# Graph edges on a clock of TensorE's work: one wait per indirect transfer, two gathers to one scatter

## The chip, the cores and the metric

The kernel runs on one core of a Trainium2 chip. The metric is device time in microseconds of one launch; the median of the runs before the change is 2226.0 us (three runs: 2226.4, 2224.77, 2226.0). The engines are named as in the profile: PE (TensorE, matrix products), PEld (its weight loads), DVE (VectorE), ACT (ScalarE), POOL (GpSimd, which here issues the indirect transfers), SP (SyncE, which issues most weight loads).

## The reference, cut to what matters

The program is a two-layer network over 625 nodes of width 1024 and 10,000 edges. The change lies in the first layer, which adds the results of a graph attention and of a linear attention to `x`. The graph attention is the part that has edges:

```python
x = x * rsqrt(mean(x*x) + EPS) * rms_w;  x = x @ W_down          # (625, 256)
xl = (x @ Wl).reshape(n, 4, 64);  xr = (x @ Wr).reshape(n, 4, 64)
msg = xl[src] + xr[dst]                                           # one row per edge
e = einsum('ehd,hd->eh', leaky_relu(msg, 0.2), att)               # 4 scores per edge
p = exp(e - segment_max(e, dst)[dst])
alpha = p / (segment_sum(p, dst)[dst] + 1e-16)
out = segment_sum(alpha[..., None] * xl[src], dst)                # then out @ W_up
```

Beside it, from the same normalised rows, runs a linear attention with four 1024x1024 matrices (`W_q`, `W_k`, `W_v`, `W_o`). A feed-forward block follows, and then a second layer with dense graph products, attention and a mixture of experts.

## The kernel before, in words

All of the first layer is written in an order made by hand (`manual_schedule`): on each engine the instructions run in the order in which the Python code emits them.

**What the edges need.** The rows of `xl` and `xr` (625 rows of 256 floats) lie in DRAM as `xl_d` and `xr_d`. The 10,000 edges are cut into 79 columns of 128 (the last has 16). Each column needs three indirect transfers, which POOL issues: a gather of 128 rows of `xl_d` (tile `ga`), a gather of 128 rows of `xr_d` (tile `gb`), both at line 611, and a scatter of the 128x4 scores into a dense DRAM `table` of 625x625x4 at line 631. That makes 237 transfers. A group is two columns (`G = 2`), so there are 40 groups. Between gather and scatter DVE scores a group: add (L621), times `att` with the rectifier (L591), sum (L592), clip (L594). ACT then takes the exponential (L598). Five pairs of `ga` and `gb` rotate, and so a gather of group g also waits until the score of group g-5 has read its tile. A scatter waits until the scatter before it has landed, as both write `table`.

**What TensorE does meanwhile.** The same stretch holds the linear attention: ten `key` and ten `value` groups (`pk`, `pv`, eight matmuls each), 79 counting steps (`pct`, five bf16 matmuls each, which count how often each pair of nodes occurs), the states (`pkv`), eight queries (`pq`) with their answers (`pd`, `po`), and the output product (`px`, in `mixed`, L745). An fp32 matmul shows as two rows in the trace. The queries' first group needs the PSUM banks that the last `value` group leaves when DVE has read it (L286).

**What sets the order of the edge work.** `one_beat` emits one beat for group g: the self loops for five of the beats, the scores of group g-`lags[0]`, the exponentials of group g-`lags[1]`, and then, for each column of the group, the gather of `ga`, a scatter of group g-`lags[2]`-1 if one is left, the gather of `gb`, and a scatter of group g-`lags[2]`. The lags are 4, 5, 6. `work(us)` is called after each piece of TensorE's work with an estimate of its time and emits a beat once the sum has passed 2.0 + 5.2 us per beat for the first six beats and 8.6 us per beat after that. Only the first transfer of a beat waits for TensorE: for the last matmul that had been emitted by then (`latest["pe"]`). Before the output product the lags become 1, 1, 2. What is left after `mixed(2)` is emitted in one go (`while chunks: one_beat()`).

**What comes next.** When all scatters have landed, POOL loads `table` back in blocks (`load_table`, tile `tb`). DVE multiplies each by the counts (`weigh`, tile `pT`, L841), and TensorE multiplies that with the rows (`sums`, `pg`). The table's columns, the feed-forward block and the second layer follow.

Of the kernel before, what the change touches and what calls it, by code (L numbers as in the profile page):

```python
# [53 lines left out]
def attempt(ctx: ExitStack, tc: tile.TileContext, w: dict, out: bass.AP, shifted: bool):  # L54

    nc = tc.nc
# [10 lines left out]
    def ps2(name):  # L67
        return psums[-1][0].tile([128, 2, 512], FP, tag="ps2", name=name, bufs=3)
# [58 lines left out]
    def group(dst, pairs):  # L127

        for i, (lhsT, rhs) in enumerate(pairs):
            made = nc.tensor.matmul(dst, lhsT=lhsT, rhs=rhs, start=(i == 0), stop=(i == len(pairs) - 1))  # L130
        latest["pe"] = made.ins.name

    latest = {}

    def behind(ins, name):

        tc.add_manual_dep(ins.ins, name, mybir.DependencyInfo(mybir.DependencyClass.Sync,
                                                              mybir.DependencyReason.DATA), reason="pace")
        return ins
# [11 lines left out]
    def nodes(t):  # L151
        return slice(t * P, (t + 1) * P)
# [203 lines left out]
    with ExitStack() as st0:  # L356
# [8 lines left out]
        with ExitStack() as edges:  # L365
# [22 lines left out]
            def load_edges():  # L388
                for dst, name in ((si, "src"), (di, "dst")):
# [15 lines left out]
                              in_=none.unsqueeze(1).to_broadcast([128, 28, 440]))  # L405
# [43 lines left out]
            def count():  # L449

                if part["held"] or part["done"] == EN:
                    return False
                lo, hi, t = counting[part["done"]]
                part["held"] = 2 * (t == hi - 1)

                def prep():
                    while len(made_ahead) < min(8, EN - t):
                        one_hot()
                    hold["hot"] = made_ahead.pop(0)
                    part["done"] += 1  # L460

                def pe():
                    od, os = hold["hot"]
                    if t == lo:
                        part["pc"] = psums[-1][0].tile([128, NT, 512], FP, tag="pct", name="pct", bufs=1)
                    for j in range(NT):
                        made = nc.tensor.matmul(part["pc"][:P, j, :HN], lhsT=os[:, nodes(j)],
                                                rhs=od[:, :HN], start=(t == lo), stop=(t == hi - 1))
                    latest["pe"] = made.ins.name

                def decode():
                    for j in range(0, NT, 2):
                        js = slice(j, min(j + 2, NT))
                        n = js.stop - j
                        low, high, v = CT[:, js, 0:HN], CT[:, js, HN:NP], part["pc"][:P, js, :HN]
                        low_r, high_r = CTr[:, js, 0:HN], CTr[:, js, HN:NP]
                        u = pool.tile([P, 2, HN], FP, tag="u", name="u", bufs=1)[:, 0:n, :]

                        nc.vector.tensor_scalar(u, v, 1728.0 if shifted else 2047.0, BIG, op0=ALU.subtract, op1=ALU.add)
                        nc.vector.tensor_scalar(u, u, BIG, None, op0=ALU.subtract)  # L480
                        if lo == 0:
                            nc.vector.tensor_tensor(low_r, v, u, op=ALU.subtract)
                            nc.vector.tensor_scalar(high_r, u, 1.0 / 4096, None, op0=ALU.mult)
                        else:
                            nc.vector.scalar_tensor_tensor(high_r, u, 1.0 / 4096, high, op0=ALU.mult, op1=ALU.add)
                            nc.vector.tensor_tensor(u, v, u, op=ALU.subtract)
                            nc.vector.tensor_tensor(low_r, low, u, op=ALU.add)
                    if hi == EN:

                        for s in range(NT):  # L490
                            nc.vector.tensor_tensor(CTr[:, s, nodes(s)], CT[:, s, nodes(s)], ident[:P, :P],
                                                    op=ALU.add)

                do(prep, pe, decode if t == hi - 1 else None)
                return True

# [103 lines left out]
            es = pool.tile([128, EN, 4], FP, name="es")  # L600
            G = 2
            groups = [(lo, min(G, EF - lo), 128) for lo in range(0, EF, G)] + [(EF, 1, ER)]
            ab = {}

            def gather(g, j, side):
                lo, n, p = groups[g]
                if j == 0 and side == 0:
                    ab[g] = [pool.tile([128, G, 256], FP, tag=k, name=k, bufs=5) for k in ("ga", "gb")]
                if j < n:
                    src, ix = ((xl_d, si), (xr_d, di))[side]  # L610
                    got = nc.gpsimd.indirect_dma_start(  # L611
                        out=ab[g][side][0:p, j, :], out_offset=None, in_=src[:, :],
                        in_offset=bass.IndirectOffsetOnAxis(ap=ix[0:p, lo + j:lo + j + 1], axis=0))
                    if j == 0 and side == 0 and "pe" in latest:
                        behind(got, latest["pe"])

            def score_group(g):
                lo, n, p = groups[g]
# [5 lines left out]
            chunks = [(g, j) for g, (lo, n, p) in enumerate(groups) for j in range(n)]  # L624

            def scatter(last):

                if chunks and chunks[0][0] <= min(last, beat["raised"] - 1):
                    g, j = chunks.pop(0)
                    lo, n, p = groups[g]  # L630
                    nc.gpsimd.indirect_dma_start(  # L631
                        out=table[:, :],
                        out_offset=bass.IndirectOffsetOnAxis(ap=at[0:p, lo + j:lo + j + 1], axis=0),
                        in_=es[0:p, lo + j, :], in_offset=None)

            own = pool.tile([P, NT, 4], FP, name="own")
            linear = pool.tile([P, NT, 4], FP, name="linear")
# [29 lines left out]

            beat = dict(us=0.0, g=0, scored=0, raised=0)  # L670
            lags = [4, 5, 6]

            def scores(last):
                while beat["scored"] <= min(last, len(groups) - 1):
# [3 lines left out]
            def raise_all(last):  # L678
                while beat["raised"] <= min(last, beat["scored"] - 1):
                    lo, n, p = groups[beat["raised"]]  # L680
                    exp(es[0:p, lo:lo + n, :])
                    beat["raised"] += 1

            def one_beat():
                g = beat["g"]
                beat["g"] += 1
                if 5 <= g < NT + 5:
                    self_loops(g - 5)
                if lags[1] > lags[0]:
                    raise_all(g - lags[1])  # L690
                    scores(g - lags[0])
                else:
                    scores(g - lags[0])
                    raise_all(g - lags[1])
                for j in range(G):
                    if g < len(groups):
                        gather(g, j, 0)
                        scatter(g - lags[2] - 1)
                        gather(g, j, 1)
                    scatter(g - lags[2])  # L700

            def work(us):
                beat["us"] += us

                while beat["us"] >= 2.0 + 5.2 * min(beat["g"], 6) + 8.6 * max(beat["g"] - 6, 0) and chunks:
                    one_beat()

            work(0.0)
            states = []
            for c in range(2):  # L710
                if c:
# [27 lines left out]
            def mixed(t, ks=range(KC), keep=None, then=None, paced=True, cs=(0, 1)):  # L739
                for c in cs:  # L740
                    def pe(c=c):
                        if c == 0 and ks[0] == 0:
                            hold["px", t] = ps2("px1")
                        for k in ks:
                            made = nc.tensor.matmul(hold["px", t][:P, c, :], lhsT=oT[:, k, nodes(t)], rhs=wo[c](k),  # L745
                                                    start=(k == 0), stop=(k == KC - 1 and keep is not None))
                        latest["pe"] = made.ins.name

                    def after():
                        px = hold.pop(("px", t))  # L750
                        for c in range(2):
                            nc.vector.tensor_tensor(keep[:, c, :], px[:P, c, :], bo[c][:P], op=ALU.add)

                    do(None, pe, after if keep is not None and c == 1 else None)
                    if then is not None and c == 0:
                        then()
                    if paced:
                        work(0.87 * len(ks))
# [29 lines left out]
            for m in range(KC):  # L788
# [5 lines left out]
                if m < 3:  # L794
# [3 lines left out]
                                      in_=w[("w_gate", "w_up", "w_down")[m]].rearrange("(k p) n -> p k n", p=128))  # L798
# [7 lines left out]
            made = [gu[:, :, 0:256], gu[:, :, 256:512], dn]  # L806
# [468 lines left out]
    for b in range(NB_MIN, NB):  # L1275
        nc.gpsimd.dma_start(out=y_d[b * 128:(b + 1) * 128, :].rearrange("p (a n) -> p a n", a=4),
                            in_=zero.unsqueeze(1).to_broadcast([128, 4, 256]))
# [694 lines left out]
```

## Time and profile before

| | us |
|---|---|
| median of three runs | 2226.0 |
| the profiled execution, its own time | 2228.76 |
| its span, as the profile draws it | 2227.0 |
| PE busy in the span | 2112.5 (95%) |
| POOL busy in the span | 341.4 (15%) |
| POOL, `ga` gathers, 79 rows | 79.7 (1009 ns each) |
| POOL, `gb` gathers, 79 rows | 81.8 (1036 ns each) |
| POOL, scatters, 79 rows | 84.2 (1066 ns each) |
| stretch 57 to 158: PE / DVE / POOL busy of 101 | 91.25 / 69.67 / 67.80 |
| stretch 158 to 259: of 101 | 99.02 / 59.60 / 66.27 |
| stretch 259 to 377: of 118 | 101.43 / 69.97 / 73.92 |
| stretch 377 to 445: of 68 | 45.57 / 41.67 / 38.37 |
| stretch 445 to 475: of 30 | 16.23 / 14.62 / 10.10 |
| stretch 475 to 640: of 165 | 147.94 / 98.86 / 5.25 |

A row of the timeline reads: start, duration, engine, line, operation, output<-inputs, count, and in brackets how long the engine sat idle before it and what ended that. "issue" means that the profile shows nothing that was waited for, "remote" a semaphore whose sender it can't name.

### The profile page before, as it was taken

How to read it: one execution, taken by the hardware profiler on the slowest of the kernel's cores; microseconds unless marked ns; L12 is line 12 of the kernel's file. 1: busy time of each engine (PE TensorE's matmuls, PEld its weight loads, DVE VectorE, ACT ScalarE, POOL GpSimd, SP SyncE). 2: the span in 40 equal slices, each digit the busy share in tenths (PEclk: the TensorE clock that was granted, in tenths of full speed). 3: DMA queues.
4: the chain of work that ended last, by engine and by line, in shares of the span. 5: the costliest groups of instructions: out<-in, count | busy, mean ns of one | idle time of the engine just before them, and what ended most of it. 6: DMA issues, size and time to landing. Idle time of an engine off the chain costs nothing. (4 is left out here: it accounts for less than half of the span.)

```text
span 2227.0 us, 17363 instructions
## 1 busy us (share of the span) xinstructions
PE 2112.5 (95%) x6934; PEld 1209.9 (54%) x6934; DVE 713.3 (32%) x1214; ACT 194.1 (9%) x354; POOL 341.4 (15%) x349
## 2 busy tenths in 40 slices
PE   8899799578899999999999999999999999999998
PEld 6466375245444777754445767557744444444443
DVE  5765467557623560000113133322011111111112
ACT  2000010001211100000000111100000000000000
POOL 1666656610000020210000000110000000000011
PEclk9999899878999999999999999999999999999999
DMA  9226252071122110231213111021099987997742
GB/s 299 77 62 209 59 182 81 25 212 33 38 85 71 52 38 1 85 142 38 76 38 104 38 38 38 20 103 61 34 347 337 331 325 282 327 331 286 275 144 92
DMA packets 145848, 301.62 MB, mean 135 GB/s; under 512 B 12370, under 2 KB 22436, under 8 KB 145754
## 3 DMA queue, kind: packets, MB, share of 16 engines
q1 hardware_dynamic: 123700, 244.23, 30.7%
q0 software_dynamic: 17376, 46.42, 7.1%
q10 hardware_dynamic: 4678, 9.72, 1.4%
q8 instruction: 58, 0.95, 0.2%
q14 instruction: 36, 0.29, 0.0%
HBM read 277.49 MB, written 22.84 MB: 135 GB/s over the span
## 5 line engine op out<-in xcount | busy, mean ns | idle before, releaser
L130 PE MATMUL pu<-w,xgT 128*128 128x512 f32 x768 | 333.9, 593 | 1.9 <-DVE xgT L1266 1.9
L130 PEld LDWEIGHTS pu<-w,xgT 128*128 128x128 f32 x768 | 144.0, 190 | 174.8 <-issue 171.7
L130 PE MATMUL pyb<-w,hb 128*128 128x512 f32 x384 | 174.3, 599 | 2.5 <-ACT yb L105 2.1
L130 PE MATMUL pq<-xnT,w 128*128 128x313 f32 x512 | 139.6, 432 | 13.8 <-DVE v L286 13.0
L130 PE MATMUL pk<-w,xnT 128*125 128x512 f32 x320 | 143.2, 599 | 3.3 <-issue 2.8
L130 PE MATMUL pv<-w,xnT 128*125 128x512 f32 x320 | 142.2, 597 | 1.5 <-issue 1.1
L130 PE MATMUL p<-tT,w 128*128 128x313 f32 x512 | 136.3, 428 | 0.4 <-DVE tT L1266 0.4
L130 PEld LDWEIGHTS pq<-xnT,w 128*128 128x128 f32 x512 | 98.2, 193 | 53.5 <-DVE v L286 13.8
L130 PEld LDWEIGHTS pyb<-w,hb 128*128 128x128 f32 x384 | 69.8, 189 | 90.9 <-issue 74.8
L1806 DVE TENSOR_TENSOR su<-pu,su 128x512 f32<-128x512 f32 x24 | 16.6, 692 | 314.6 <-ACT su L1805 314.6
L130 PEld LDWEIGHTS p<-tT,w 128*128 128x128 f32 x512 | 96.8, 190 | 37.9 <-issue 1.2
L130 PEld LDWEIGHTS pk<-w,xnT 128*125 128x125 f32 x320 | 59.8, 189 | 77.0 <-issue 76.1
L130 PEld LDWEIGHTS pv<-w,xnT 128*125 128x125 f32 x320 | 59.9, 189 | 75.4 <-issue 72.6
L1789 POOL DMA_INDIRECT xg<-rows_d,slots x12 | 11.4, 946 | 524.8 <-PE pxg L1796 449.0
L631 POOL DMA_INDIRECT table<-es,at x79 | 84.2, 1066 | 49.4 <-issue 26.2
L611 POOL DMA_INDIRECT ga<-xl_d,si x79 | 79.7, 1009 | 74.8 <-issue 33.2
L611 POOL DMA_INDIRECT gb<-xr_d,di x79 | 81.8, 1036 | 25.3 <-issue 22.8
L745 PE MATMUL px<-w,oT 128*125 128x512 f32 x160 | 69.8, 594 | 2.9 <-DVE x L909 2.0
L130 PE MATMUL px<-w,hT 128*125 128x512 f32 x160 | 70.3, 592 | 0.0
L130 PE MATMUL px<-w,oT 128*125 128x512 f32 x160 | 70.3, 592 | 0.0
L130 PE MATMUL ph<-meanT,w 128*128 128x313 f32 x256 | 70.1, 426 | 0.0
L130 PE MATMUL ph<-xnT,w 128*128 128x313 f32 x256 | 70.0, 427 | 0.0
(366 smaller groups left out, 2459.9 us busy)
## 6 DMA issues: line engine op xcount, KB each, us to landing
w<-in_eW_dram SPq DMA_DIRECT2D x144, 1024.0 KB
w<-in_L_Wk_dram SPq DMA_DIRECT2D x8, 1024.0 KB
w<-in_L_Wv_dram SPq DMA_DIRECT2D x8, 1024.0 KB
w<-in_L_Wq_dram SPq DMA_DIRECT2D x8, 1024.0 KB
w<-in_L_Wo_dram SPq DMA_DIRECT2D x8, 1024.0 KB
w<-in_W_self_dram SPq DMA_DIRECT2D x8, 1024.0 KB
w<-in_W_neigh_dram SPq DMA_DIRECT2D x8, 1024.0 KB
w<-in_sW_dram SPq DMA_DIRECT2D x8, 1024.0 KB
```

Of the source, the lines that this page charges most:

```text
L130: made = nc.tensor.matmul(dst, lhsT=lhsT, rhs=rhs, start=(i == 0), stop=(i == len(pairs) - 1))
L611: got = nc.gpsimd.indirect_dma_start(out=ab[g][side][0:p, j, :], out_offset=None, in_=src[:, :], in_offset=bass.IndirectOffsetOnAxis(ap=ix ...
L631: nc.gpsimd.indirect_dma_start(out=table[:, :], out_offset=bass.IndirectOffsetOnAxis(ap=at[0:p, lo + j:lo + j + 1], axis=0), in_=es[0:p, l ...
L745: made = nc.tensor.matmul(hold["px", t][:P, c, :], lhsT=oT[:, k, nodes(t)], rhs=wo[c](k), start=(k == 0), stop=(k == KC - 1 and keep is no ...
L1789: nc.gpsimd.indirect_dma_start(out=xg, out_offset=None, in_=rows_d[:, :], in_offset=bass.IndirectOffsetOnAxis(ap=slots[:, b:b + 1], axis=0))
L1806: nc.vector.tensor_tensor(su, pu[:, 0, :], su, op=ALU.mult)
```

## The change

A clock of TensorE's work is kept while the program is emitted: every matmul adds its estimated time to `pe_time` and leaves a mark (`passed`). A 128x512 fp32 matmul counts 0.87 us, one of 313 columns 0.53, one of the counting step 0.135. Each of the 237 transfers now gets its own wait (`in_time`): for the first matmul whose mark has reached `due`, which starts 1.5 us after the first mark of the stage and grows by 1.38 us with each transfer. A beat holds, for each column, the gather of `ga`, the gather of `gb` and one scatter; the second scatter is gone. The lags are 2, 3, 5 and still become 1, 1, 2 ahead of the output product. `work` emits a beat once the clock has passed the due times of all its transfers, and its argument is no longer read.

```diff
@@ group, and the clock
+            passed(made, 0.0017 * max(dst.free_size(), 154))
-        latest["pe"] = made.ins.name
-
-    latest = {}
+    pe_time = [0.0]
+    marks = []
+
+    def passed(made, us):
+        pe_time[0] += us
+        marks.append((pe_time[0], made.ins.name))
@@ count
-                    latest["pe"] = made.ins.name
+                        passed(made, 0.135)
@@ gather
-                    if j == 0 and side == 0 and "pe" in latest:
-                        behind(got, latest["pe"])
+                    in_time(got)
@@ scatter
-                    nc.gpsimd.indirect_dma_start(
+                    in_time(nc.gpsimd.indirect_dma_start(
...
-            beat = dict(us=0.0, g=0, scored=0, raised=0)
-            lags = [4, 5, 6]
+            beat = dict(g=0, scored=0, raised=0, due=pe_time[0] + 1.5)
+            lags = [2, 3, 5]
+
+            def in_time(made):
+                name = next((name for us, name in marks if us >= beat["due"]), None)
+                if name is not None:
+                    behind(made, name)
+                beat["due"] += 1.38
@@ one_beat
                     if g < len(groups):
                         gather(g, j, 0)
-                        scatter(g - lags[2] - 1)
                         gather(g, j, 1)
                     scatter(g - lags[2])
@@ work
-                beat["us"] += us
-                while beat["us"] >= 2.0 + 5.2 * min(beat["g"], 6) + 8.6 * max(beat["g"] - 6, 0) and chunks:
+                while chunks and pe_time[0] >= beat["due"] + 1.38 * (4 * (beat["g"] < len(groups)) + 2 * (beat["g"] > lags[2])):
                     one_beat()
-            work(0.0)
@@ mixed
-                        latest["pe"] = made.ins.name
+                            passed(made, 0.87)
```

`behind(ins, name)` is unchanged: it makes `ins` wait for the named instruction.

More of the change, by code (lines that the diff above doesn't have):

```diff
@@ L630, in scatter @@
                     lo, n, p = groups[g]
-                    nc.gpsimd.indirect_dma_start(
+                    in_time(nc.gpsimd.indirect_dma_start(
                         out=table[:, :],
                         out_offset=bass.IndirectOffsetOnAxis(ap=at[0:p, lo + j:lo + j + 1], axis=0),
-                        in_=es[0:p, lo + j, :], in_offset=None)
+                        in_=es[0:p, lo + j, :], in_offset=None))
             own = pool.tile([P, NT, 4], FP, name="own")
```

## The prediction

> **What bounds the kernel now.** I read the busy times by stretch first, to find where PE stands still, then PE's timeline around those places, then POOL's timeline over the same time. PE is the bound (95% of the span). In the stage of the edges it works from 45.01 us (first `pk`) to 422.57 (end of the `px` row below), and its next matmul waits:
>
> ```profile
> 394.86 27.71 PE L745 MATMUL px<-w,oT 128*125 128x512 f32 x64
> 454.23 0.68 PE L130 MATMUL pg<-xl,pT 125*125 125x65 f32 x2 [31.66 <-DVE pT L841]
> ```
>
> The `pT` that it waits for needs the loaded table, and the table needs the last scatter. POOL's timeline shows how late the transfers end:
>
> ```profile
> 384.86 0.96 POOL L611 DMA_INDIRECT ga<-xl_d,si  x1 [8.50 <-PE px L745]
> ...
> 422.00 1.12 POOL L631 DMA_INDIRECT table<-es,at  x1 [0.75 <-issue]
> 423.43 2.29 POOL L611 DMA_INDIRECT gb<-xr_d,di  x1 [0.30 <-issue]
> 426.02 1.73 POOL L631 DMA_INDIRECT table<-es,at  x1 [0.30 <-issue]
> 429.67 1.56 POOL L631 DMA_INDIRECT table<-es,at  x1 [1.91 <-ACT es L598]
> 432.64 2.31 POOL L631 DMA_INDIRECT table<-es,at  x1 [1.41 <-DMA table<-es,at]
> 436.82 0.96 POOL L631 DMA_INDIRECT table<-es,at  x1 [1.88 <-issue]
> 439.18 0.96 POOL L631 DMA_INDIRECT table<-es,at  x1 [1.39 <-DMA table<-es,at]
> 442.03 0.85 POOL L631 DMA_INDIRECT table<-es,at  x1 [1.90 <-issue]
> 444.54 0.90 POOL L173 DMA_DIRECT2D tb<-table  x1 [1.66 <-issue]
> ```
>
> Two numbers follow. From 422.00 to 442.03 there are seven steps of 2.86 us, as each scatter waits for the one before it. From the last scatter to the first `pg` it is 454.23 - 442.03 = 12.2 us. The first row shows why the end is late: with 32 transfers still to come after it, POOL is made to wait 8.50 us for a beat.
>
> The second loss lies inside the stage. By the change's own clock (read off the code) PE's work from the first `pk` to the last `px` is 344.1 us; the trace has 422.57 - 45.01 = 377.6. So 33.4 us are lost, 13.0 of them in one place:
>
> ```profile
> 252.29 7.03 PE L130 MATMUL pv<-w,xnT 128*125 128x512 f32 x16
> 272.33 10.21 PE L130 MATMUL pq<-xnT,w 128*128 128x313 f32 x32 [13.01 <-DVE v L286]
> ```
> ```profile
> 271.59 0.69 DVE L286 TENSOR_TENSOR v<-pv,bv_t 125x512 f32<-125x512 f32 x1 [12.73 <-remote]
> ```
> ```profile
> 267.61 0.99 POOL L631 DMA_INDIRECT table<-es,at  x1 [0.30 <-issue]
> 271.82 0.96 POOL L611 DMA_INDIRECT ga<-xl_d,si  x1 [3.23 <-remote]
> ```
>
> By its rows the `pv` group ended at 259.3, yet DVE, which only needs that group here, starts 12.3 us later, and POOL's wait ends with it. PE's signals arrive late. The same shows at 80.67, 227.01 and 351.75 (6.9, 11.1 and 3.6 us late). Each time POOL had issued for 21 to 40 us with gaps of 0.44 or less, and the signal came 2.1 to 3.0 us after POOL's last row. At 77 to 81 and 99 to 110 PE's own rows stretch to one per 0.7 or 1.4 us. Whether POOL's unbroken run holds the signals back, or only waits for them too, this trace can't tell.
>
> **The change, part by part.** *Earlier places.* In the built program the last gather waits for clock 312.6, where before it waited for 330.2; transfer 227, the last that has a gather just ahead of it, waits for 313.4. With PE's loss unchanged that is 45.0 + 313.4 + 33.4 = 391.8, and 1.0 for its turn gives 392.8.
>
> *Can POOL keep up?* From 57 to 376 there are 204 transfers, busy 207.8 us, with 0.30 between rows: 1.32 us each against 1.38 on the clock. The first starts at 57.64 in both (it waits for the rows of `xl_d`), so 227 end at 57.6 + 299.6 = 357.2, and some 19 us of waits for landings and scores in that stretch make 376. That leaves 16 us to 391.8, so TensorE's clock decides, not POOL.
>
> *The tail.* The extra scatter is gone, so scatters stay five groups behind and ten stand alone after transfer 227 (before, seven). 10 x 2.86 = 28.6, so the last starts at 421.4. The row-to-row bounds are 2.36 (436.82 to 439.18) and 4.18 (432.64 to 436.82), that is 24 to 42 us; I take the mean of the seven. DVE's three ternary passes (11.2 us) fall on this tail as they did before, so their effect is in the mean. [...] The rows agree: 1.56 to 2.31 us for a transfer beside those passes, 0.85 to 0.96 after them. Were all ten to fall under the passes, at (432.64 - 426.02)/2 = 3.3 a step, the sum would be 4.5 us higher.
>
> *From the last scatter on.* 421.4 + 12.2 = 433.6 for the first `pg`, against 454.23: 20.6 us less. PE still idles 11.0 us. Its granted clock was 0.78 from 420 to 430 and 0.50 until 470, and an 11 us gap cools it too, so no gain is counted for a warm start. What follows moves as a whole, as its loads start from these same events.
>
> *Shorter lags.* A score stands two beats after its gathers instead of four. Two beats and the beat's own 8.28 us, less 5.5 to the fourth gather and about 4 for issue and landing, leave 15 us of cover. POOL starts 11 us behind its places (57.64 against 46.5), and in the weight loads near 180 a scatter takes 6.8 to 7.3 us (169.41, 176.18, 183.48) against 4.14 on the clock. If the lag passes 15 us, DVE stands at the add, with `kb`, `kf` and `v` behind it in its queue and PE behind those. I price it at 0, bounds 0 and 5. Exponentials one beat after scores let ACT wait less; no price.
>
> *The waits.* On POOL's queue everything behind a waiting transfer waits too: other transfers, one memset, at the end the table loads. PE's signals in the stage rise from 117 to 331 (counted in the built program). A signal has no visible price: counting rows with one per five matmuls take 4.16/30 = 0.139 us against 0.135 on the clock, so at most 214 x 0.02 = 4 us, at least 0; I take 0. The 91 more wait instructions on POOL: rows with several waits show the same 0.30 gap as rows with none (98.12, 60.58), and 16 us of cover stand over them. [...]
>
> *PE's 33.4 us.* POOL now stops at the first late signal instead of running on to its next beat. At 259 it issued seven rows after the group had ended. If the signal comes 3 us after POOL's last row and POOL stops at once, 12.3 us late becomes about 4, which saves 8. I take half, 4.0, since POOL often lags and then runs on. Bounds: a saving of 16.8 (beyond it POOL's 376 decides) and a loss of 33.4 (as much again).
>
> **Sum.** 2227.0 - 20.6 - 4.0 = 2202.4 for a span. The median stands 1.0 below the span here (the execution's own 2228.76 stands 1.8 above), so **2201**.
>
> **The rivals.** *Signals come in time* (0.17): pauses spread over all transfers end the late signals. POOL then decides: 376 + 1 + 28.6 + 12.2 = 417.8 for `pg`, 36.4 less, a median of 2190. For it: no late signal from 158 to 195, where POOL has gaps of 1 to 4 us. Against: the new gaps are 0.06 us on average.
>
> *The scatter chain takes the place* (0.15): POOL drops behind in the weight loads (about 3 us per scatter, as above) and doesn't recover at 0.06 a transfer, and transfer 227 comes 10 to 17 us late: 2211 to 2218. Against: PE's losses give POOL time.
>
> *TensorE is held back more, slower* (0.25): before, a beat ended in a pause when POOL was on time; now POOL rests 0.06 us per transfer. If an unbroken run is what makes signals late, then 327 us at one episode per 22 us are 15 episodes. The six so far cost 5.6 each; at 4 each the loss is 60, 27 us more: 2226 - 20.6 + 27 = 2232. It decides from a loss of 54 us (33.4 + 20.6). Against: each wait stops POOL at once, and 384.86 to 422, a transfer per 1.6 us, shows no late signal.
>
> *The change doesn't do what it says*: in the built program all 237 transfers wait for a matmul, in steps of 0.9 to 1.9 us of the clock. Dropped.
>
> **How the numbers follow.** My forecast has 0.43; its own range is 2194 to 2208. No change is what a measurement can't tell, within 0.2% or 4.5 us; it takes 0.03 from the scatter chain and 0.03 from the slow case. Faster is 0.43 + 0.17 + 0.12 = 0.72, same 0.06, slower 0.22. The range reaches down to the first rival with scatters at 2.5 a step (2186) and up to the slow case with some more loss: 2184 to 2238.
>
> **What would show it.** Last gather near 389, last scatter near 417, first `pg` near 430, with some 11 us of idle PE before it instead of 31.66; no transfer waiting longer than about 3 us but for signals or landings; lone scatters 2.4 to 3.3 apart. Wrong would be: PE's end of `px` well past 423, rows one per 0.7 or 1.4 us in many places, or DVE's L621 waiting for gathers before 380.

## The result and the profile after

| | before | after |
|---|---|---|
| median of 12 runs each, us | 2226.20 (2222.62 to 2229.49) | 2225.33 (2220.86 to 2232.87) |
| ratio, 95% interval | | 1.0002 (0.9989 to 1.0014) |
| profiled execution: span, us | 2227.0 | 2228.1 |
| end of `px` before the first `pg` | 422.57 | 438.87 |
| TensorE's loss (that end, less the first `pk`, less 344.1) | 33.5 | 49.7 |
| start of transfer 227 / last scatter | 417.83 / 442.03 | 412.37 / 443.80 |
| first `pg`, and PE's idle time before it | 454.23, 31.66 | 455.76, 16.89 |

There is no difference that can be told from none; 25 us less were forecast. Later runs on other chips show that this is not the whole answer: on a chip where the kernel before takes 2196 us the change is slower, 1.0060 (1.0040 to 1.0079).

PE's timeline of the changed kernel at the end of the stage (start, duration, engine, line, operation, count, idle time before it and what ended that):

```profile
411.16 27.71 PE L753 MATMUL px<-w,oT 128*125 128x512 f32 x64
455.76 0.68 PE L130 MATMUL pg<-xl,pT 125*125 125x65 f32 x2 [16.89 <-DVE pT L849]
```

The idle time before `pg` is halved, as intended, but `px` ends 16.3 us later, and `pg` starts 1.5 us later than before. POOL's timeline of the same kernel shows the lone scatters:

```profile
410.75 1.32 POOL L617 DMA_INDIRECT gb<-xr_d,di  x1 [0.30 <-issue]
412.37 1.02 POOL L636 DMA_INDIRECT table<-es,at  x1 [0.30 <-issue]
415.28 0.97 POOL L636 DMA_INDIRECT table<-es,at  x1 [1.89 <-PE px L753]
418.16 1.94 POOL L636 DMA_INDIRECT table<-es,at  x1 [1.91 <-ACT es L604]
421.96 1.85 POOL L636 DMA_INDIRECT table<-es,at  x1 [1.86 <-issue]
...
443.80 0.85 POOL L636 DMA_INDIRECT table<-es,at  x1 [1.95 <-DMA table<-es,at]
446.31 0.89 POOL L179 DMA_DIRECT2D tb<-table  x1 [1.66 <-issue]
```

Transfer 227 starts 5.5 us earlier than before, but the ten steps behind it take 31.4 us (3.14 each) for 24.2 before, because eleven scatters stand alone behind the last gather (410.75), for six before. From the last scatter to `pg` it is 12.0 us.

Where did PE lose 16.3 us more? The windows give, for a stretch, the busy time of PE, PEld, DVE, ACT and POOL with their counts, PE's granted clock, the DMA share and GB/s. Before:

```profile
150.00:250.00 100.00, 95.92 (x358) 55.28 (x357) 56.96 (x126) 8.84 (x25) 63.74 (x64) 1.00 0.44 145
360.00:390.00 30.00, 29.13 (x77) 14.09 (x76) 23.81 (x18) 1.55 (x3) 16.00 (x16) 1.00 0.30 97
```

After:

```profile
150.00:250.00 100.00, 86.57 (x306) 48.46 (x305) 53.49 (x120) 7.68 (x22) 67.27 (x66) 0.91 0.44 145
360.00:390.00 30.00, 21.77 (x61) 12.98 (x62) 17.45 (x17) 3.31 (x7) 17.91 (x19) 0.83 0.33 104
```

PE is busy 9.4 and 7.4 us less in these two stretches, and its granted clock falls to 0.91 and 0.83 in them. What stands behind the gaps, in the timelines of PE, DVE and ACT after the change:

```profile
233.81 1.01 PE L130 MATMUL pk<-w,xnT 128*125 128x512 f32 x1 [1.79 <-issue]
280.81 4.44 PE L130 MATMUL pq<-xnT,w 128*128 128x313 f32 x9 [13.53 <-DVE v L292]
368.23 11.15 PE L130 MATMUL pq<-xnT,w 128*128 128x313 f32 x32 [9.24 <-ACT qf L338]
```

```profile
181.44 0.69 DVE L626 TENSOR_TENSOR ga<-ga,gb 128x512 f32<-128x512 f32 x1 [7.46 <-DMA gb<-xr_d,di]
217.93 0.69 DVE L626 TENSOR_TENSOR ga<-ga,gb 128x512 f32<-128x512 f32 x1 [5.28 <-DMA gb<-xr_d,di]
```

Two things are mixed here. Around 233 single `pk` rows stand up to 1.8 us apart, and the idle times that end at 280.81 and 368.23 follow signals of PE that reach DVE and ACT late (their rows wait 9.85 and 18.05 us for "remote"). The kernel before has such episodes too. A further gap, 4.84 us for 0.29 before, ends at 171.47, where PE waits for its weights; the 16 `pk` rows behind it take 8.80 us, for 7.10 before, at a granted clock of 0.81 (171.4 to 180.3). New are the two DVE rows: a score waits for its own gather. Nine scores do so between 64 and 218 us, 35.6 us together; before, none did until `px` was well under way (409.76). The experiments had to part the two.

### The profile page after: what moved, and what is told of

Read it like the earlier page. It is cut to its first block, busy times and chain, and to the rows that moved or that the text cites. A ratio compares the mean times of both kernels' runs of the same rounds, so it can differ in the third digit from the quotient of the medians.

```text
span 2228.1 us, 17452 instructions
## 1 busy us (share of the span) xinstructions
PE 2117.1 (95%) x6934; PEld 1212.4 (54%) x6934; DVE 711.0 (32%) x1214; ACT 193.9 (9%) x354; POOL 342.1 (15%) x349
## 5 line engine op out<-in xcount | busy, mean ns | idle before, releaser
L130 PE MATMUL pq<-xnT,w 128*128 128x313 f32 x512 | 143.0, 439 | 22.8 <-DVE v L292 13.5
L130 PE MATMUL pk<-w,xnT 128*125 128x512 f32 x320 | 148.3, 615 | 12.5 <-issue 7.4
L130 PEld LDWEIGHTS pq<-xnT,w 128*128 128x128 f32 x512 | 100.0, 196 | 64.1 <-DVE v L292 14.4
L1814 DVE TENSOR_TENSOR su<-pu,su 128x512 f32<-128x512 f32 x24 | 16.6, 692 | 314.6 <-ACT su L1813 314.6
```

Source lines behind the costliest of these rows:

```text
L1814: nc.vector.tensor_tensor(su, pu[:, 0, :], su, op=ALU.mult)
```

## The experiments

"Loss" is TensorE's loss as in the table above. "First chip" and so on number the four chips that the runs fell on: e1 to e4 on the first, e5 to e8 on the second, e9 to e16 on the third, e17 and e18 on the fourth. Which chip made the two profiles above is not recorded; its time for the kernel before is the first chip's.

### Does the loss come from the transfers? (first chip)

The first three leave transfers of the groups from the sixth on out, but keep their places on the clock; the table is then incomplete or zero, other experts are chosen further on (13 expert blocks for 12 in e1 and e2), and only the stage is compared.

```diff
@@ e1, e2: scatter
+                    if g >= 5:
+                        beat["due"] += 1.38
+                        return
@@ e1, e3: gather
+                if j < n and g >= 5:
+                    beat["due"] += 1.38
+                elif j < n:
@@ e3: scatter, data
-                        in_=es[0:p, lo + j, :], in_offset=None))
+                        in_=es[0:p, lo + j, :] if g < 5 else none[0:p, 0:4], in_offset=None))
```

> Leaves out the gathers and scatters of groups 5 to 39 (207 of 237 transfers); their places on the clock, the scores and every other instruction stay. PE's loss is the time from the first pk row to the end of the last px row, less 344.1 us: 33.4 before, 49.7 after the change. Theory A, the stream of indirect transfers holds TensorE back: loss under 12 us, all of it near the start, and no late signal after 110 us; the span falls to about 2170 to 2180, as nothing is waited for at the tail either. Theory B, the loss comes from the other work of the stage (DVE's, the weight loads, code loading): loss stays at 30 to 50 us, span 2190 to 2210.

> Leaves out the scatters of groups 5 to 39 (69 of 79); all gathers stay at their places on the clock, so POOL has a pause of 1.4 us and more after each two. Theory A1, any unbroken stream of indirect transfers does it: the pauses end it, loss under 12 us. Theory A2, the gathers do it (1 KB to each of 128 partitions): loss stays at 30 to 50 us. Theory A3, the scatters do it (128 pieces of 16 bytes into DRAM, each waiting for the one before): loss under 12 us too, and e3 tells A3 from A1.

> Leaves out the gathers of groups 5 to 39 and scatters zeros there, at the scatters' places on the clock: one transfer in 4.14 us. A1 and A2: loss under 12 us. A3: loss stays at 30 to 50 us.

| | transfers in the stage | loss | first `pg` | time |
|---|---|---|---|---|
| the change | 237 | 49.7 | 455.76 | 2229.98 (this execution) |
| e1, neither | 30 | 3.6 | 392.54 | 2207.62 |
| e2, gathers alone | 168 | 11.3 | 400.27 | 2213.07 |
| e3, scatters of zeros alone | 99 | -2.0 | 401.58 | 6379.67, as the zeros make the kernel's second attempt run |

PE's timeline of e1:

```profile
364.99 27.71 PE L760 MATMUL px<-w,oT 128*125 128x512 f32 x64
392.54 2.62 PE L130 MATMUL pg<-xl,pT 125*125 125x65 f32 x23
```

No idle time is left before `pg`, and no late signal shows behind the last of the 30 transfers (132.61). So on this chip the loss needs the transfers. In e3 no row waits for "remote": scatters alone cost TensorE nothing (-2.0), the gathers alone, with pauses in the scatters' places, 11.3, and both together some 50.

### Do the waits cost? (first chip)

```diff
@@ in_time: only a beat's first transfer waits (40 waits for 237)
-                if name is not None:
+                if name is not None and beat.pop("first", None):
```

> The change with a wait on TensorE only for the first transfer of each beat: order, lags and clock as in the change, 40 waits in place of 237. If the 237 waits and TensorE's many more signals cost the 16.3 us by which PE's loss grew (theory C): loss back to about 33 us, last scatter about 16 us earlier, 2209 to 2215 us. If they don't (theory D, the loss is the transfers' and a matter of where the episodes fall): loss 40 to 55 us, 2220 to 2235 us.

Measured: 2223.71 (2215.36 to 2234.80), ratio to before 0.9991 (0.9972 to 1.0009); loss 40.5, first `pg` at 446.55. Its late signals lie elsewhere (151 to 170, 252 to 256, 278 to 289), and VectorE waits 1.1 us for a gather in one place. The time cannot be told from either kernel's, so the price of the waits stays open; the loss is there with 40 waits as with 237.

### The same kernel on another chip, and three sizes (second chip)

```diff
@@ e5: nothing
@@ e6
-            lags = [2, 3, 5]
+            lags = [4, 5, 6]
@@ e7: also in work()
-                beat["due"] += 1.38
+                beat["due"] += 1.60
@@ e8
-            lags = [2, 3, 5]
+            lags = [2, 2, 3]
```

> The changed kernel itself, unaltered, for a second profile. Theory 'the stream holds TensorE back' (the lot of the indirect transfers, one behind the other, delays TensorE's work in episodes whose places are not set by the program): TensorE's loss (end of the last px row before the first pg, less the start of the first pk, less 344.1) is again between 40 and 58 us, but its episodes fall at other places than 227-241, 267-281 and 359-368. Rival 'a fixed wait of the program': loss 49.7 within 3 us, with idle rows at the same three places.

> The changed kernel with the lags set back from 2, 3, 5 to 4, 5, 6; the clock and two gathers to one scatter stay. Rival 'the shorter lags' (VectorE meets gathers that have not landed, and TensorE waits for VectorE): the loss falls from 49.7 to 33-38 us. Theory 'the stream': the loss stays between 40 and 58 us. Both: 12 lone scatters in place of 10 at the end, 2 x 3.14 = 6.3 us, so the first pg is at 455.76 + 6.3 = 462 for the stream and at 446-450 for the lags; the time 2226-2237 for the stream and 2214-2221 for the lags.

> The changed kernel with 1.60 us of TensorE's clock between transfers in place of 1.38. Theory 'the stream' as a matter of how close the transfers stand (11.3 us of loss with the gathers alone, 49.7 with all): loss between 12 and 30 us. Rival 'a fixed price for every transfer': (342.5 / 1.60) = 214 transfers in the stage for 227, loss 49.7 x 214 / 227 = 47, not under 40. Both: at the end of the clock 23 transfers are left, of them some 14 scatters at 3.14 us and 9 gathers at 1.3 us, 57 us behind TensorE's end, so the first pg near 414 + 57 + 12 = 483 by the one and near 505 by the other; the kernel is slower either way and only the loss tells them apart.

> The changed kernel with lags 2, 2, 3 for 2, 3, 5: 6 lone scatters at the end for 10. If the loss is the stream's and stays near 50 us: first pg 4 x 3.14 = 12.6 us earlier, at 443, and a time of 2213 (2207-2220). Rival 'the shorter lags': the scatter comes sooner behind its score, POOL waits for it, the loss or the gaps of POOL grow by 8 us or more, and the time stays at 2221-2232.

This chip upset every number: the kernel before took 2196.22 us on it. No engine waits for "remote" anywhere in the stage.

| | loss | last scatter | first `pg` | VectorE's waits for gathers before 360 us | time, ratio to before |
|---|---|---|---|---|---|
| e5, the change | 15.4 | 422.49 | 434.40 | 19, 71.5 us | 2209.48 (one run) |
| e6, lags 4, 5, 6 | 8.0 | 424.80 | 436.67 | 3, 4.9 us | 2212.91, 1.0068 (1.0051 to 1.0085) |
| e7, 1.60 us | -3.0 | 432.14 | 443.69 | 1, 2.9 us | 2220.85 (one run) |
| e8, lags 2, 2, 3 | 18.5 | 415.56 | 427.54 | 13, 49.5 us | 2202.31, 1.0026 (1.0015 to 1.0037) |

Both theories of e5 fell: the loss is not 40 to 58 and not 49.7. The gathers' waits come in sight instead, since nothing hides them now. But e6 warns: with the old lags they are gone, and yet the time is no better. And e8 has the largest loss and the best time of the four. The time goes with the last scatter, not with the loss.

### The two kernels side by side (third chip)

> The kernel before itself, unaltered, profiled on the same chip as the next three. The second set ran on another chip than the first: the kernel before took 2196.22 us there for 2226 us, and the clock granted to TensorE in the changed kernel's windows was 0.97 to 1.00 there for 0.91 to 0.97. Theory 'the stream is what costs, and the chip says how much': where the kernel before takes about 2196 us its loss is near 0 (not over 6) and its first pg near 421, which is 434.4 less the 13.3 us by which one run of the change was longer; where it takes about 2226 us, loss near 33 and first pg near 454. Rival 'the chips differ elsewhere': the loss is 25 or more in either case and the difference lies behind the first pg.

> The changed kernel itself, unaltered, timed beside the run before it. On a chip where the kernel before takes about 2196 us: the change is slower by 8 to 16 us, ratio 1.004 to 1.007, with a loss of 10 to 20 and the first pg near 434. On a chip where it takes about 2226 us: ratio 0.998 to 1.002 with a loss of 35 to 55. Rival 'the one run of 2209.48 was an outlier': ratio within 0.002 of 1 on either chip.

The chips differ in this very stage: the kernel before has a loss of -3.0 here, and its first `pg` is at 418.77 for 454.23, 35.5 us earlier, where its whole span is 33.1 us shorter. PE's timeline of the kernel before (e9), and of the change (e10):

```profile
358.69 27.71 PE L745 MATMUL px<-w,oT 128*125 128x512 f32 x64
418.77 0.68 PE L130 MATMUL pg<-xl,pT 125*125 125x65 f32 x2 [32.37 <-DVE pT L841]
```

```profile
377.76 27.71 PE L753 MATMUL px<-w,oT 128*125 128x512 f32 x64
434.49 0.68 PE L130 MATMUL pg<-xl,pT 125*125 125x65 f32 x2 [29.02 <-DVE pT L849]
```

The change: 2211.31, ratio 1.0060 (1.0040 to 1.0079); `px` ends 19.1 us later, `pg` starts 15.7 us later. In e10 the loss can be followed row by row. DVE's timeline:

```profile
234.45 0.68 DVE L292 TENSOR_TENSOR v<-pv,bv_t 125x512 f32<-125x512 f32 x1
239.77 0.69 DVE L626 TENSOR_TENSOR ga<-ga,gb 128x512 f32<-128x512 f32 x1 [4.64 <-DMA gb<-xr_d,di]
...
242.02 0.68 DVE L271 TENSOR_TENSOR kb<-pk,bk_t 125x512 f32<-125x512 f32 x1
247.53 0.69 DVE L626 TENSOR_TENSOR ga<-ga,gb 128x512 f32<-128x512 f32 x1 [4.84 <-DMA gb<-xr_d,di]
...
250.38 0.68 DVE L292 TENSOR_TENSOR v<-pv,bv_t 125x512 f32<-125x512 f32 x1
```

and PE's, of the same kernel:

```profile
235.19 7.03 PE L130 MATMUL pv<-w,xnT 128*125 128x512 f32 x16
251.12 9.26 PE L130 MATMUL pq<-xnT,w 128*128 128x313 f32 x26 [8.91 <-DVE v L292]
```

PE has finished `pv` at 242.2, but DVE reads it at 250.38, because `kb` and two scores, each waiting for its gather, stand before it in DVE's queue. PE needs the bank and idles 8.91 us. In e9 PE finishes `pv` at 241.3, DVE reads it at 241.34, and PE waits 0.78.

From the end of a group's last gather (`gb`, second column) to the start of its score the rows give the cover. In e9 it is 6 to 31 us up to group 35; in e10 it is 1.7 to 1.9 us in 13 of the 20 groups from 10 to 29, which is all that landing takes, so DVE waits there. At 244.88 POOL issues transfer 127, whose place on the clock is 45.1 + 1.5 + 126 x 1.38 = 220.5, while TensorE is only 0.9 us behind e9 by then: POOL is 24 us late, and a lag of two beats (16.6 us) is used up.

### The three parts alone (third chip)

```diff
@@ e13, the clock alone: the change, with
-            lags = [2, 3, 5]
+            lags = [4, 5, 6]
...
                         gather(g, j, 0)
+                        scatter(g - lags[2] - 1)
                         gather(g, j, 1)
@@ e14, the lags alone: the kernel before, with
-            lags = [4, 5, 6]
+            lags = [2, 3, 5]
@@ e16, the order alone: the kernel before, with
-                        scatter(g - lags[2] - 1)
@@ e11: the change with the second scatter back; e12: that, lags 2, 2, 3, and 1.45 for 1.38
@@ e15: e13 with 1.43 for 1.38
```

> The changed kernel with the second scatter put back between the two gathers (the 'two gathers to one scatter' undone; clock and lags stay): 6 transfers in the last lone run for 11, so 5 scatters cost a place of 1.38 in the stream for a lone step of 3.14. Theory: tail 5 x 1.76 = 8.8 us shorter, first pg 8.8 us earlier than in the changed kernel, ratio to it 0.996. Rival 'TensorE gives it back': the loss grows by as much as the tail shrinks, and the time is the changed kernel's within 3 us.

> The changed kernel with the second scatter back, lags 2, 2, 3, and 1.45 us of the clock for each transfer in place of 1.38: 237 x 1.45 = 344, so the stream lasts as long as TensorE's work in the stage. Theory 'the loss goes with how close the transfers stand' (1.60 gave a loss of -3.0 on the second chip, 1.38 gave 15.4): loss 0 to 8 on a chip like the second, 15 to 35 on one like the first; few lone scatters, first pg 12 to 20 us before the changed kernel's; time 2188 to 2198 or 2206 to 2216, faster than both kernels. Rival 'the lone tail comes back': transfers pushed past TensorE's end are run at 3.14 us each, first pg no earlier than in the changed kernel.

> The clock alone: the changed kernel with lags 4, 5, 6 and the second scatter back between the gathers. Theory 'the scores two beats behind stand in VectorE's queue before their gathers have landed': no wait of VectorE for a gather over 2 us before 360 us, TensorE's loss -3 to 3 on a chip where the kernel before takes 2196 us (33 or so where it takes 2226), 8 lone scatters for 6, first pg within 6 us of the kernel before, ratio to it 0.997 to 1.003. Rival 'the clocked stream holds TensorE back whatever the lags': loss 10 or more above the kernel before's, ratio 1.004 or more.

> The lags alone: the kernel before with lags 2, 3, 5 for 4, 5, 6. In the kernel before a score stands 7 to 30 us behind its last gather; two beats of 8.6 us less leave under 1.9 us, the time to landing, in about half of the groups. Theory: VectorE waits for gathers in 10 to 20 groups before 360 us, 30 to 75 us in all, loss 8 to 20 us above the kernel before's, 5 lone scatters for 6, ratio 1.002 to 1.008. Rival 'the clock is what costs': fewer than 10 us of such waits, loss within 4 us of the kernel before's, ratio 0.998 to 1.001.

> The clock alone with 1.43 us for each transfer, the 8.6 us for six of the kernel before, in place of 1.38 (lags 4, 5, 6, second scatter back). Theory: 6 lone scatters as in the kernel before, loss as there within 3 us, stream as there or 1 to 5 us earlier since each transfer waits for its own place only; ratio 0.996 to 1.001. Rival 'the clocked stream': ratio 1.004 or more.

> The order alone: the kernel before without its second scatter between the two gathers. 13 lone scatters at the end for 6: 7 x (3.14 - 1.38) = 12.3 us on the tail, loss as in the kernel before within 2 us, first pg 12 us later, ratio 1.0055 (1.004 to 1.007). Rival 'the tail is hidden': ratio within 0.001 of 1.

| third chip | loss | transfer 227 | last scatter | first `pg` | ratio to before |
|---|---|---|---|---|---|
| e9, before | -3.0 | 382.82 | 406.86 | 418.77 | |
| e16, order alone | 0.6 | 386.50 | 415.07 | 427.04 | 1.0026 (1.0015 to 1.0038) |
| e14, lags alone | 15.2 | 394.87 | 417.21 | 428.95 | 1.0029 (1.0020 to 1.0038) |
| e13, clock alone | 13.0 | 395.15 | 422.51 | 434.56 | 1.0052 (1.0036 to 1.0068) |
| e15, clock alone at 1.43 | -3.4 | 395.65 | 419.18 | 430.70 | 1.0047 (1.0030 to 1.0064) |
| e11, clock and lags | 16.1 | 393.71 | 417.79 | 430.24 | 1.0027 (1.0015 to 1.0038) |
| e12, e11 with lags 2, 2, 3 at 1.45 | 10.7 | 398.30 | 419.88 | 431.95 | 1.0047 (1.0030 to 1.0064) |
| e10, all three | 16.3 | 390.87 | 422.53 | 434.49 | 1.0060 (1.0040 to 1.0079) |

Each of the three parts alone makes this chip's kernel slower, and the intervals of all three lie above 1. Their shifts of `pg` (15.8, 10.2 and 8.3 us) sum to 34.3, all together give 15.7: they do not add, and shorter lags take back a part of what the clock costs (`pg` 430.24 with both, 434.56 with the clock alone).

*The lags* do what e10 suggested. With them alone VectorE waits 57.6 us for gathers in 15 places before 360, and the loss is 18.2 us above the kernel before's. Only 10.2 of that reach `pg`; the idle time before it shrinks from 32.4 to 24.8.

*The order* costs two thirds of what the tail's arithmetic said: `pg` comes 8.3 us later, for 12.3 expected, and the ratio of 1.0026 lies below the expected range.

*The clock* was expected to be harmless, and is not. Two causes show. In e13 12.61 us of loss are one place, at the switch of the lags to 1, 1, 2:

```profile
359.80 13.98 PE L754 MATMUL px<-w,oT 128*125 128x512 f32 x32
386.39 13.94 PE L754 MATMUL px<-w,oT 128*125 128x512 f32 x27 [12.61 <-DVE kept L761]
```

DVE's timeline there has a score in front of `kept`:

```profile
382.77 0.69 DVE L626 TENSOR_TENSOR ga<-ga,gb 128x512 f32<-128x512 f32 x1 [10.30 <-DMA gb<-xr_d,di]
...
385.05 0.69 DVE L761 TENSOR_TENSOR kept<-px,bk_t 125x512 f32<-125x512 f32 x1
```

With 1.43 that place is gone (loss -3.4), but the transfers are as late, and `pg` only 3.9 us earlier. They fall behind at the first scatters. POOL's timeline of e15:

```profile
88.43 1.03 POOL L617 DMA_INDIRECT gb<-xr_d,di  x1 [0.30 <-issue]
94.08 1.00 POOL L636 DMA_INDIRECT table<-es,at  x1 [4.63 <-PE pk L130]
...
104.84 0.99 POOL L636 DMA_INDIRECT table<-es,at  x1 [3.43 <-PE pv L130]
```

and of the kernel before (e9), the same three transfers (26, 27 and 33):

```profile
88.83 0.95 POOL L611 DMA_INDIRECT gb<-xr_d,di  x1 [0.30 <-issue]
90.09 1.01 POOL L631 DMA_INDIRECT table<-es,at  x1 [0.30 <-issue]
...
99.07 1.13 POOL L631 DMA_INDIRECT table<-es,at  x1 [1.64 <-ACT xl L663]
```

The releaser that e15's rows name is misleading: the places of these transfers on the clock, 45 + 1.5 + 1.43 x 26 = 83.7 and 45 + 1.5 + 1.43 x 32 = 92.3, are long past at 94.08 and 104.84. Their own scores are ready as well: the exponential of group 0 ended at 84.81, that of group 1 at 92.48. What such a scatter also waits for is the self loops' write into the same `table` (`table<-own`), which ACT issues in the same beat; in e17 (below) the row of transfer 33 names it. ACT's timeline of e15 has the write ahead of transfer 33:

```profile
102.70 0.41 ACTq L180 DMA_DIRECT2D table<-own  x1
```

In e9 that write is issued at 96.49. The one ahead of transfer 27 is issued at 91.81, in e9 at 83.41, and there transfer 27 waits for nothing. The scores stand later too: 16.0, 18.9 and 21.6 us behind the gathers of groups 0, 1 and 2, for 6.3, 6.7 and 12.6 in e9. `work` used to emit a beat when its time began; now it does so when the due times of all its transfers have passed. Self loops, scores and exponentials so move about a beat later in the queues of DVE and ACT, the first scatters with them, and transfer 33 is 5.8 us late. It grows to 9.9 by transfer 81, in the weight loads, and is 12.8 at transfer 227; what adds the later part was not followed.

e11 and e12 were meant to be the better version. e11 is faster than the change, as expected (2203.45 us for 2211.31), though its `pg` comes only 4.3 us earlier for 8.8. Neither beats the kernel before, and e12 has no earlier `pg` than e11: with 1.45 the stream ends later.

### Waits or places? (fourth chip)

```diff
@@ e17: e15 with a wait at a beat's first transfer alone
-                if name is not None:
+                if name is not None and beat.pop("first", None):
```

> The clock at 1.43 us with lags 4, 5, 6 and the second scatter back, and a wait for TensorE at the first transfer of each beat alone. Theory 'a wait at every transfer holds POOL back, since one late place is never made up': transfer 33 and the ones behind it are 4 to 12 us earlier than in e15, last scatter within 4 us of the kernel before's, ratio to it 0.998 to 1.002. Rival 'the placing of the beats does it': the stream is that of e15, last scatter 8 to 14 us behind the kernel before's, ratio 1.003 to 1.006.

> The kernel before, unaltered, profiled beside e17 on its chip: transfer 33 near 99 and the last scatter near 407 where it takes 2196 us.

This chip is like the first: the kernel before takes 2232.91 us, with a loss of 33.6 and `pg` at 454.83. e17 takes 2239.47 in the median, ratio 1.0007 (0.9982 to 1.0032), which settles nothing of the time: four of its twelve executions take 2224.5 to 2226.6 us, eight 2234 to 2246. The first scatters do tell: transfer 33 starts at 111.62 for 104.17 in e18, 7.4 us late with 40 waits, where e15 was 5.8 late with 237. POOL's row:

```profile
111.62 1.02 POOL L636 DMA_INDIRECT table<-es,at  x1 [3.44 <-DMA table<-own]
```

So the places of the beats delay the first scatters, as the rival had it, and not the waits. The end of the stream tells less: the last scatter starts 14.4 us behind e18's, but the profiled execution of e17 (2246.18 us) is one of the longest of its twelve. Its loss is 52.9, with no wait for a gather before 360: on such a chip TensorE loses 40 to 53 us in every clocked version with all its transfers that was profiled (three kernels, one execution each), the lags long or short.

## Why the prediction was wrong

Against the profile after, the forecast of the first `pg`, 429.6 with the saving on the loss, misses by 26.2 us: 20.3 the loss, 3.2 the place of transfer 227, 2.8 the tail, -0.2 the rest of the chain, 0.1 the start.

- **"PE's 33.4 us", priced at a saving of 4.0: the step that failed.** It became 49.7, 16.2 more. The mechanism that the step assumed, POOL stopping at once at a late signal, is not what happened: between 267.3, where the rows of the last `pv` group end, and 280.06, where DVE reads it, POOL still issued eight transfers (before, in the like place, seven). POOL ran late: it issued transfer 138 at 272.64, whose place without loss is 45.1 + 1.5 + 137 x 1.38 = 235.7, and TensorE was 26 us late by then (its last `pv` rows end at 267.3, for 241.3 in e9), so POOL was some 11 us behind by this estimate, and most of the marks that it waited for lay in the past. The episodes were no shorter: 12.6 us at 227 to 241, 13.5 at 281, 9.2 at 368. What makes the signals late stays open. The bound of the step (a loss as large again) held, and the rival "TensorE is held back more" had the direction; its point of decision, a loss of 54, was missed by 4, which is why the time is equal and not slower. The size is that of one execution, 4.7 us above its kernel's median (the one before: 2.6 above), so by an estimate from these numbers, if the excess lies in this stage, the two kernels' usual losses lie nearer 14 than 16 us apart.
- **"Shorter lags", priced at 0 (0 to 5): failed too.** The mechanism stands in the prediction, and its sign was named: a score waiting for gathers before 380. The 4 us that it takes for issue and landing are 2.9 to 3.7 in the rows of the kernel before (gather at 406.84, score at 409.76; 423.43 and 427.17). The cover of 15 us took POOL's lateness as the 11 us of its start, and it grows: in e10 it was 16 at transfer 70, 25 at transfer 81, beside the weight loads, and 24 at transfer 127. The prediction had seen the slow scatters in the weight loads (6.8 to 7.3 us) and gave them no price here. Alone the lags cost 18.2 us of loss and 10.2 of `pg` on the third chip, 1.0029. How much of the 16.2 on the first chip is theirs was not tried by itself; e4 and e17 have a loss of 40.5 and 52.9 almost without such waits, so a loss of this size needs none.
- **"Can POOL keep up?", 376 for transfer 227, so TensorE's clock decides: failed where signals come in time.** On the third chip it was 382.82 for the kernel before and 390.87 for the change. There POOL and the scores that it waits for set the end, and an earlier place on the clock brings nothing. On the first chip the place did decide: 45.1 + 313.4 + 49.7 = 408.2, and transfer 227 started 4.2 us behind it, for 1.0 taken.
- **Left out of the sum:** that `work` emits a beat after its due times, not ahead of them. The prediction counts it as cover for the scores ("the beat's own 8.28 us") and not as a delay of the first scatters. The clock alone costs 12 to 16 us of `pg` on the third chip.
- **The tail** was right as a mechanism and 10% short: ten steps of 3.14 us for 2.86, inside the bounds of 24 and 42. The term was mis-sized by a reading: of the seven steps from 422.00 to 442.03 one is a gather's (423.43), and only six scatters stood alone; from 426.02 to 442.03 the same rows give 16.01/5 = 3.20 a step. Transfers 229 to 231 take 1.94, 1.85 and 1.80 us beside DVE's ternary passes (417.45 to 428.68), and 0.96 once these are over. On the third chip the tail takes 31.7, for 24.0 before, and the order alone, with 13 scatters at the very end for 6, moves `pg` by 8.3.
- **From the last scatter on, 12.2 us: right.** 12.0 after the change, 11.5 to 12.5 in every other run with all its transfers. The granted clock behind the gap is 0.50 up to 470 us, after 16.89 us of idle PE as after 31.66, and it was 0.50 behind shorter gaps inside the stage too (13.01 us before, from 272 to 274; 9.24 after, from 368 to 372), so no warm start shows. That the rest moves as a whole is right as well: from `pg` to the end of the span it is 1772.8 before and 1772.3 after, 1775.1 in e9 and 1775.3 in e10.
- **"Signals come in time"** was a rival with 2190. The second and third chip show that very case, and the kernel before gains more from it (2226 to 2196 us) than the change does (2225 to 2211); transfer 227 at 390.87, for the 376 of that rival, is the larger part of its miss.
- **The waits**, priced at 0: nothing in e4 or e17 speaks against it, and neither can confirm it.

The forecast time also had a premise that one trace cannot show: that the 33.4 us belong to the kernel. They belong to the kernel on some chips.

## What to carry to other kernels

VectorE worked its queue in order here (in e10 `v` at 250.38 stood behind a score that waited 4.84 us), so a helper's work that is emitted a fixed number of beats behind a transfer is only hidden while the issuing engine is on time: measure the cover, from the end of the issue to the start of the use, in every group, and subtract the lateness that grows, not the one at the start. When a stage ends with the last of a chain of transfers, follow that chain first; TensorE's loss here moved by 18 us while the end moved by 10. And before a stall is ascribed to a program, profile the same program on a second chip.

## What the runs showed of the hardware

- The same program differs by chip: 2226 to 2233 us on two, 2196 on two others, and the difference lies in the 400 us in which 237 indirect transfers run beside TensorE. On the former, matmul rows thin out to one per 0.7 to 2.8 us, and other engines' waits for PE end up to 13 us after PE's rows have; without the transfers such a chip loses 3.6 us (e1), and without the gathers nothing (-2.0, e3). On the latter the same transfers cost nothing (-3.0). Why the chips differ stays open.
- A gather's rows were usable 1.9 us after its issue row had ended, and 4 to 6 us in the weight loads between 158 and 190 (e10).
- The releaser that the trace names for a wait on several semaphores can be one that was due some 10 us before (e15's first scatter: place 83.7, start 94.08); only the other conditions of the instruction show the true one, there the landing of another engine's write into the same table.
